# A pair-product batch norm: loads, shift, squares and root of its head rearranged

## The chip, the core and the metric

The kernel runs on one core of one Trainium2 chip. The metric is the device time of one execution in microseconds (us). The kernel before takes 1929.05 us, the median of three runs that lie between 1929.01 and 1929.15.

## The reference, cut to what matters

```python
# xi, xj: 1024 x 39 x 16; W: 1 x 16 x 16; 741 pairs (row > col)
cross = xj[:, rows, :, None] * xi[:, cols, None, :]          # 1024 x 741 x 16 x 16
mean = jnp.mean(cross, axis=(0, 2, 3), keepdims=True)        # one per pair
var = jnp.mean(jnp.square(cross - mean), axis=(0, 2, 3), keepdims=True)
normed = (cross - mean) * jax.lax.rsqrt(var + BN_EPS) * gamma + beta
out = normed * W
```

The output is 776.99 MB in float32, so that storing it takes nearly all the time. The statistics of a pair come from sums per field: both mean and variance follow from 39x39 matrices of products of sums of x and of x squared. To keep the variance exact, a shift per field is subtracted first.

## The kernel before

On each partition lie eight samples (t = 0 to 7). A head computes the statistics and at the same time prepares the first two output tiles as unscaled products. A long plateau then makes tile after tile: ScalarE and GpSimd multiply, VectorE adds and weighs with W, SP stores. The parts that the change and the argument touch:

```python
for t0 in range(0, NT, T):                                   # loads, two samples each
    nc.sync.dma_start(xj_sb[:, t0:t0+T], ...); nc.scalar.dma_start(xi_sb[:, t0:t0+T], ...)
nc.gpsimd.dma_start(w_sb[:, 0, :], ...)                      # W, on GpSimd's queue
# ... gamma on SP, beta on ScalarE's queue
sums(0)                                                      # VectorE: sums of samples 0, 1
emit(raw0, 8)                                                # ScalarE: eight products of tile 0
nc.scalar.copy(w_dve, w_sb)                                  # W to PSUM, for VectorE
# matmuls over the partitions -> shift (ScalarE)
for n in range(7): deviation(n)                              # GpSimd: x - shift
for n in range(8):
    square(n)                                                # ScalarE
    emit(raw0, 3)
    # ... VectorE: sums, moments(n), means(n); after two n: gram matmuls
emit(raw_products(1, nc.gpsimd, range(20, 32)), 12)
emit(raw1, 6)
# ... ScalarE: gram copies;  emit(raw1, 6);  VectorE: 15 steps on 39x39, reciprocal
nc.scalar.activation(rstd, inv, AF.Sqrt)                     # the root
emit(raw1, 8)
# ... VectorE: last steps; spread() by matmul to all partitions, then
#     st = ps * gamma ; st[1] = st[1] + beta    (the second: an addition with two SBUF inputs)
affine(0); weigh(0, FIRST_PIECES); scale_xi(2); spread(..); spread(..); affine(1); weigh(1, ..)
# ... three more spreads, then the loop over tiles: finish(2) is the first VectorE work of the plateau
```

`affine` alternates its 19 columns between ScalarE and GpSimd; `weigh` is VectorE's product with W, followed by a store of each piece.

## Time and profile before

| | kernel before |
|---|---|
| time | 1929.05 us |
| busy: VectorE, ScalarE, GpSimd | 90%, 86%, 79% of the span |
| DMA | busy without a break from 100 to 1650 us at 420 GB/s |
| first square on ScalarE | 15.59 us |
| gram copies | 37.84 us |
| affine operations, ScalarE | 45.88 us |
| third tile's finishing begins | 75.87 us |

Shares of busy time average over two stages with quite different limits, so they say little here. The DMA is the limit of the plateau. What a change of the head can win is how much earlier the plateau begins; this is the last line of the table. The prediction shows the lines.

### The profile page before, as it was taken

To read this page: it belongs to the slowest core of one execution; us is meant where nothing else is said; L and a number is where in the kernel's file an instruction comes from. 1 tells how busy PE (TensorE), PEld (TensorE's weight loads), DVE (VectorE), ACT (ScalarE), POOL (GpSimd) and SP (SyncE) were. 2 spreads that over 40 slices of the span, in tenths; PEclk is the share of its full clock that TensorE was granted. 3 is DMA by queue.
4 is the path that set the end of the run, shared out by engine and by line. 5 is a ranking of instruction groups with operands and counts; after the bars stand their busy time and mean duration, and the time that the engine had idled before them with its cause. 6 is when DMAs were issued, how large, how long until landed. Compare 5 with 4: busy or idle time off the path is not lost. (4 is left out here: it accounts for less than half of the span.)

```text
span 1927.5 us, 10086 instructions
## 1 busy us (share of the span) xinstructions
PE 25.5 (1%) x132; PEld 23.8 (1%) x132; DVE 1732.3 (90%) x2603; ACT 1663.4 (86%) x3690; POOL 1528.2 (79%) x1918
## 2 busy tenths in 40 slices
PE   2200000000000000000000000000000000000000
PEld 2200000000000000000000000000000000000000
DVE  5999999999989899999999999999999999888886
ACT  7999888888888988889888898888888888888752
POOL 6898888887878787979787878888888877777654
DMA  3799999999999999999999999999999999999998
GB/s 125 326 421 421 420 421 421 421 421 421 424 426 423 424 425 423 426 423 426 423 421 421 421 421 416 411 420 416 414 415 414 415 414 415 405 406 402 393 389 373
DMA packets 80174, 783.66 MB, mean 407 GB/s; under 512 B 4800, under 2 KB 5824, under 8 KB 14816
## 3 DMA queue, kind: packets, MB, share of 16 engines
q1 hardware_dynamic: 79328, 779.95, 96.8%
q10 hardware_dynamic: 720, 2.94, 0.4%
q14 instruction: 77, 0.63, 0.1%
q0 software_dynamic: 48, 0.13, 0.1%
q8 instruction: 1, 0.02, 0.0%
HBM read 6.00 MB, written 776.99 MB: 406 GB/s over the span
## 5 line engine op out<-in xcount | busy, mean ns | idle before, releaser
L222 DVE SCALAR_TENSOR_TENSOR y_sb<-y_sb,st_sb,w_dve 128x512 f32<-128x512 f32 x2542 | 1679.7, 742 | 158.5 <-issue 147.1
L130 ACT ACTIVATE y_sb<-xs,xj_sb 128x256 f32<-128x256 f32 (+33 forms) x3600 | 1613.4, 542 | 218.7 <-DMA out_dram<-y_sb 166.2
L132 POOL TENSOR_SCALAR y_sb<-xs,xj_sb 128x256 f32<-128x256 f32 (+33 forms) x1200 | 604.3, 527 | 198.5 <-DMA out_dram<-y_sb 131.3
L214 POOL TENSOR_TENSOR y_sb<-y_sb,w_sb 128x1024 f32<-128x1024 f32 (+4 forms) x138 | 441.8, 3202 | 11.5
L150 POOL TENSOR_TENSOR xs<-xi_sb,st_sb 128x576 f32<-128x576 f32 (+37 forms) x150 | 188.0, 1253 | 146.4 <-ACT y_sb L130 146.4
L210 POOL TENSOR_SCALAR y_sb<-y_sb,st_sb 128x512 f32<-128x512 f32 x384 | 259.6, 693 | 1.7 <-ACT y_sb L130 1.7
L130 ACT ACTIVATE y_sb<-xi_sb,xj_sb 128x304 f32<-128x304 f32 x52 | 23.9, 533 | 0.0
L191 DVE TENSOR_TENSOR y_sb<-y_sb,w_dve 128x5120 f32<-128x5120 f32 (+3 forms) x5 | 20.9, 4205 | 3.2 <-ACT y_sb L181 3.2
L183 POOL TENSOR_SCALAR y_sb<-y_sb,st_sb 128x512 f32<-128x512 f32 x18 | 13.5, 772 | 7.5 <-DVE st_sb L396 7.5
L383 PE MATMUL ps<-y_sb 39*128 39x38 f32 (+37 forms) x76 | 16.9, 398 | 20.1 <-DVE st_sb L390 13.9
L383 PEld LDWEIGHTS ps<-y_sb 39*128 39x128 f32 x76 | 16.4, 328 | 20.7 <-DVE st_sb L390 14.2
L281 DVE TENSOR_REDUCE y_sb<-y_sb 128x78 f32<-128x1248 f32 x8 | 11.6, 1448 | 3.8 <-ACT y_sb L275 3.6
L266 POOL TENSOR_TENSOR y_sb<-xj_sb,y_sb 128x1248 f32<-128x1248 f32 x4 | 9.3, 2321 | 6.3 <-ACT y_sb L319 6.3
L181 ACT ACTIVATE y_sb<-y_sb,st_sb 128x512 f32<-128x512 f32 x20 | 14.2, 798 | 0.0
L260 DVE TENSOR_REDUCE y_sb<-xj_sb 128x78 f32<-128x1248 f32 x4 | 5.8, 1449 | 8.5 <-DMA xj_sb<-in_r_xj_dram 8.5
L275 ACT ACTIVATE y_sb<-y_sb 128x1248 f32<-128x1248 f32 x8 | 9.8, 1228 | 2.2 <-POOL y_sb L266 2.2
L266 POOL TENSOR_TENSOR y_sb<-xi_sb,y_sb 128x1248 f32<-128x1248 f32 x4 | 9.3, 2318 | 0.0
L130 ACT ACT_TABLE_LOAD x1 | 1.3, 1283 | 7.8 <-DMA xi_sb<-in_r_xi_dram 7.8
L298 PE MATMUL ps_g<-y_sb 128*39 128x79 f32 x48 | 7.2, 339 | 18.6 <-DVE y_sb L286 18.6
L298 PEld LDWEIGHTS ps_g<-y_sb 128*39 128x39 f32 x48 | 6.1, 183 | 19.5 <-POOL y_sb L266 11.2
L132 POOL TENSOR_SCALAR y_sb<-xi_sb,xj_sb 128x304 f32<-128x304 f32 x12 | 5.9, 509 | 0.0
L260 DVE TENSOR_REDUCE y_sb<-xi_sb 128x78 f32<-128x1248 f32 x4 | 5.8, 1442 | 0.0
(42 smaller groups left out, 23.3 us busy)
## 6 DMA issues: line engine op xcount, KB each, us to landing
out_dram<-y_sb SPq DMA_DIRECT2D x56, 3072.0 KB, 11.7
out_dram<-y_sb SPq DMA_DIRECT2D x56, 2816.0 KB, 13.7
out_dram<-y_sb SPq DMA_DIRECT2D x52, 2560.0 KB, 14.2
out_dram<-y_sb SPq DMA_DIRECT2D x32, 3328.0 KB, 16.5
out_dram<-y_sb SPq DMA_DIRECT2D x16, 3584.0 KB, 17.8
out_dram<-y_sb SPq DMA_DIRECT2D x23, 2304.0 KB, 15.6
out_dram<-y_sb SPq DMA_DIRECT2D x20, 2048.0 KB, 22.4
out_dram<-y_sb SPq DMA_DIRECT2D x8, 1792.0 KB, 18.9
```

The lines of the kernel that those rows point to most:

```text
L130: nc.scalar.activation(y, src, AF.Copy, scale=scale)
L132: engine.tensor_scalar(y, src, scale, 1.0, ALU.mult, ALU.mult)
L150: nc.gpsimd.tensor_tensor(xs, xi_sb[:, t0 : t0 + T, 0:r, :], s_sb[:, :, n0 : n0 + r, :].to_broadcast([P, T, r, E]), ALU.mult,)
L181: nc.scalar.activation(y[:, :, c, :], y[:, :, c, :], AF.Identity, bias=t_c, scale=s_c)
L183: nc.gpsimd.tensor_scalar(y[:, :, c, :], y[:, :, c, :], s_c, t_c, ALU.mult, ALU.add)
L191: nc.vector.tensor_tensor(y[:, :, c0:c1, :], y[:, :, c0:c1, :], w_dve.unsqueeze(1).to_broadcast([P, T, c1 - c0, EE]), ALU.mult,)
L210: nc.gpsimd.tensor_scalar(y[:, :, c, :], y[:, :, c, :], t_sb[:, n0 + c : n0 + c + 1], 1.0, ALU.add, ALU.mult)
L214: nc.gpsimd.tensor_tensor(y[:, :, split:r, :], y[:, :, split:r, :], w_sb.unsqueeze(1).to_broadcast([P, T, r - split, EE]), ALU.mult,)
L222: stt(y[:, :, c, :], y[:, :, c, :], t_sb[:, n0 + c : n0 + c + 1], w_dve.to_broadcast([P, T, EE]), ALU.add, ALU.mult,)
L266: nc.gpsimd.tensor_tensor(devs[n % 7], sources[x][:, t0 : t0 + T], shift[:, x : x + 1, :].unsqueeze(3).to_broadcast([P, T, F, E]), ALU.sub ...
L298: nc.tensor.matmul(acc[0:F, 0 : 2 * F + 1], lhs, fb[:, t], start=t == 0, stop=t == NT - 1)
L383: nc.tensor.matmul(ps_v[:, :, first[r] - n0 : first[r] - n0 + r], pick[:, r, :], stq[:, :, 0:r], start=True, stop=True,)
```

## The change

The intent: let the statistics begin with the first sample alone (half-size first loads, shift from one sample), keep W's load from disturbing the loads of the fields, load only one activation table (an early dummy root brings in the table that also holds the copies and squares), and place products in ScalarE's gaps.

```diff
-FIRST_PIECES = (0, 3, 9, 19)
+FIRST_PIECES = (0, 2, 8, 19)
+LOADS = (0, 1, 2, 4, 6, 8)
...
-        for t0 in range(0, NT, T):
-            (loads of two samples)
-        nc.gpsimd.dma_start(w_sb[:, 0, :], ...)
+        for t0, t1 in zip(LOADS, LOADS[1:]):
+            (loads of t0 to t1)
+        nc.sync.dma_start(w_sb[:, 0, :], ...)
...
-        raw1 = raw_products(1, nc.scalar, range(20))
-        sums(0)
-        emit(raw0, 8)
-        nc.scalar.copy(w_dve, w_sb)
-        (shift from two samples)
+        raw1 = raw_products(1, nc.scalar, range(17))
+        nc.scalar.activation(shift_r, ones[0:F, 0:1], AF.Sqrt)
+        sums(0, 1)
+        (shift from one sample)
...
         for n in range(7):
             deviation(n)
+        emit(raw0, 4)
+        nc.scalar.copy(w_dve, w_sb)
         for n in range(2 * NT // T):
             square(n)
-            emit(raw0, 3)
+            emit(raw0, 4 if n < 4 else 3)
             (sums and means moved ahead)
-        emit(raw_products(1, nc.gpsimd, range(20, 32)), 12)
-        emit(raw1, 6)
+        emit(raw_products(1, nc.gpsimd, range(17, 32)), 15)
+        emit(raw1, 4)
         (gram copies)
-        emit(raw1, 6)
+        emit(raw1, 7)
         (39x39 steps, root)
-        emit(raw1, 8)
+        emit(raw1, 6)
```

More of the change, by code (lines that the diff above doesn't have):

```diff
@@ L232, in tile_pair_outer_batchnorm @@
     with tc.manual_schedule():
-        for t0 in range(0, NT, T):
-            nc.sync.dma_start(xj_sb[:, t0 : t0 + T], xj_v[:, t0 : t0 + T])
-            nc.scalar.dma_start(xi_sb[:, t0 : t0 + T], xi_v[:, t0 : t0 + T])
-        nc.gpsimd.dma_start(w_sb[:, 0, :], w.rearrange("o i j -> (o i j)").partition_broadcast(P))
+        for t0, t1 in zip(LOADS, LOADS[1:]):
+            nc.sync.dma_start(xj_sb[:, t0:t1], xj_v[:, t0:t1])
+            nc.scalar.dma_start(xi_sb[:, t0:t1], xi_v[:, t0:t1])
+        nc.sync.dma_start(w_sb[:, 0, :], w.rearrange("o i j -> (o i j)").partition_broadcast(P))
         nc.sync.dma_start(gb_all[:, 0], gamma.partition_broadcast(P))
@@ L246, in tile_pair_outer_batchnorm @@
         )
-        k_s = 1.0 / (T * P * E)
+        k_s = 1.0 / (P * E)
         batches = range(0, NT, T)
@@ L256, in part, with sums @@
             return slice(x * F, (x + 1) * F)
-        def sums(t0):
+        def sums(t0, t1):
             for x in range(2):
                 nc.vector.tensor_reduce(
-                    total[:, t0 : t0 + T, part(x)], sources[x][:, t0 : t0 + T], AX.X, ALU.add
+                    total[:, t0:t1, part(x)], sources[x][:, t0:t1], AX.X, ALU.add
                 )
@@ L302, in tile_pair_outer_batchnorm @@
         raw0 = raw_products(0, nc.scalar, range(32))
-        raw1 = raw_products(1, nc.scalar, range(20))
-        sums(0)
-        emit(raw0, 8)
-        nc.scalar.copy(w_dve, w_sb)
-        for t in range(T):
-            nc.tensor.matmul(
-                ps_s[:, 0 : 2 * F], ones, total[:, t], start=t == 0, stop=t == T - 1
-            )
-        for t in range(T):
-            nc.tensor.matmul(
-                ps_r[0:F, 0:1], total[:, t, 0:F], ones[:, 0:1], start=t == 0, stop=t == T - 1
-            )
+        raw1 = raw_products(1, nc.scalar, range(17))
+        nc.scalar.activation(shift_r, ones[0:F, 0:1], AF.Sqrt)
+        sums(0, 1)
+        nc.tensor.matmul(ps_s[:, 0 : 2 * F], ones, total[:, 0], start=True, stop=True)
+        nc.tensor.matmul(ps_r[0:F, 0:1], total[:, 0, 0:F], ones[:, 0:1], start=True, stop=True)
         nc.scalar.activation(
@@ L321, in tile_pair_outer_batchnorm @@
         nc.scalar.copy(ps_u, shift)
-        sums(2)
+        sums(1, 2)
+        means(0)
+        means(1)
         for n in range(7):
             deviation(n)
+        emit(raw0, 4)
+        nc.scalar.copy(w_dve, w_sb)
         for n in range(2 * NT // T):
             square(n)
-            emit(raw0, 3)
-            if n % 2 == 1 and n < 5:
-                sums(n + 3)
+            emit(raw0, 4 if n < 4 else 3)
+            if n % 2 == 0 and n < 6:
+                sums(n + 2, n + 4)
             moments(n)
@@ L332, in tile_pair_outer_batchnorm @@
                 deviation(7)
-            means(n)
+            if n % 2 == 0 and n < 6:
+                means(n + 2)
+                means(n + 3)
             if n % 2 == 1:
                 gram(n // 2 * T)
-        emit(raw_products(1, nc.gpsimd, range(20, 32)), 12)
-        emit(raw1, 6)
+        emit(raw_products(1, nc.gpsimd, range(17, 32)), 15)
+        emit(raw1, 4)
         for to, acc in zip((g1, g2, g3), ps_g):
```

## The prediction

> **What bounds the kernel now.** I first read the page's slices, then the table of engines and DMA by stretches of time. The core writes 776.99 MB, and between 100 and 1650 us the DMA engines are busy all the time at about 420 GB/s: that is the plateau. The time is therefore the length of the plateau and a tail, plus what comes before the stores flow without a gap. In the stretches, the columns after the engines are the clock, the share of DMA time and GB/s:
>
> ```profile
> 76.00:78.00 2.00, 0.00 (x0) 0.00 (x0) 2.00 (x4) 2.00 (x6) 2.00 (x5) 1.00 0.99 415
> 78.00:80.00 2.00, 0.00 (x0) 0.00 (x0) 2.00 (x4) 2.00 (x6) 2.00 (x3) 1.00 0.05 19
> 80.00:82.00 2.00, 0.00 (x0) 0.00 (x0) 2.00 (x4) 2.00 (x6) 1.92 (x3) 1.00 0.00 0
> 82.00:84.00 2.00, 0.00 (x0) 0.00 (x0) 2.00 (x4) 2.00 (x6) 2.00 (x3) 1.00 0.61 253
> ```
>
> See that the stores of the first two tiles run dry at 78 us, and nothing moves until the third tile's first piece is finished at about 82. So no earlier byte helps by itself: what counts is when VectorE begins the third tile's finishing operations (75.87 us in the timeline). From there it is 100% busy until 250 us. It makes 262 KB each 0.659 us (16 of them take 10.55 us between 75.87 and 86.4), 398 GB/s; GpSimd adds its 13% of the columns, so production barely exceeds the 421 GB/s that leave. **The end should move by as much as 75.87 moves.**
>
> Next, the timeline of the first 76 us, backwards from there. These lines carry it (start, length, engine, line, operation):
>
> ```profile
> 12.64 0.36 ACT L306 COPY w_dve<-w_sb 128x256 f32<-128x256 f32 x1
> 13.24 2.32 POOL L266 TENSOR_TENSOR y_sb<-xj_sb,y_sb 128x1248 f32<-128x1248 f32 x1 [6.25 <-ACT y_sb L319]
> 15.59 1.24 ACT L275 ACTIVATE y_sb<-y_sb 128x1248 f32<-128x1248 f32 x1 [2.17 <-POOL y_sb L266]
> ...
> 32.76 1.23 ACT L275 ACTIVATE y_sb<-y_sb 128x1248 f32<-128x1248 f32 x1
> ...
> 35.66 1.80 PE L298 MATMUL ps_g<-y_sb 128*39 128x79 f32 x12 [2.39 <-DVE y_sb L286]
> 37.84 0.45 ACT L344 ACTIVATE y_sb<-ps_g 39x79 f32<-39x79 f32 x3
> ...
> 40.94 1.28 ACT L368 ACT_TABLE_LOAD   x1
> 42.23 0.23 ACT L368 ACTIVATE y_sb<-y_sb 39x39 f32<-39x39 f32 x1
> ...
> 45.88 14.20 ACT L181 ACTIVATE y_sb<-y_sb,st_sb 128x512 f32<-128x512 f32 x20
> ...
> 53.13 5.49 DVE L191 TENSOR_TENSOR y_sb<-y_sb,w_dve 128x5120 f32<-128x5120 f32 x1 [0.17 <-ACT y_sb L181]
> ...
> 58.86 0.99 DVE L396 TENSOR_TENSOR st_sb<-st_sb,y_sb 128x66 f32<-128x66 f32 x1
> ```
>
> The reader is to see three stages. (1) Squares: GpSimd makes eight deviations (2.27 us apart), ScalarE squares each and puts three products behind it. The squares start every 2.455 us (15.59, 18.05, 20.50, ... 32.76), and ScalarE shows no wait after 15.59: ScalarE sets the pace, not GpSimd. (2) The small chain: gram products, the 39x39 steps, the root. (3) ScalarE's twenty affine operations start at 45.88 although their input was ready at 44.78: ScalarE was late with its products. From 53.13 VectorE has no wait of weight until 75, so 75.87 moves rigidly with it.
>
> **What the Trainium skill says.** "DMA: Bandwidth & Descriptors", section "Queues, rings and completion order": SP and ACT each own one ring on each of the same 16 DMA engines, and descriptors are consumed in ring order. The trace agrees: gamma was issued behind the fields at 7.28 us and took 11.9 us, to 19.2, whereas DMA work had ended at about 18.4; so a small load waits for all before it, and a landing shows 0.8 us after the last byte. "ScalarE: Activation LUTs", section "What ACT_TABLE_LOAD costs": about 1283 ns for the load, plus a drain of about 1380 ns. The trace shows 1.28 us, and the next operation 1.29 us after the load's start (40.94 to 42.23): no further drain is visible here, so I use 1.29. "SBUF — State Buffer", section "Who interferes with whom": a VectorE operation with two SBUF inputs is blocked by a GpSimd operation that reads SBUF. The 0.99 us at 58.86 agrees: a like addition on 110 elements, more than its 66, took 0.28 us at 60.17; GpSimd was in its affine operations until 59.66.
>
> **The change, part by part.**
>
> *Loads.* The first loads are halves (0.32 MB each). In the trace 0.205 MB have moved by 3.0 us, and the rate is then some 415 GB/s, so the first pair (0.64 MB) is through at about 4.1 and lands at 4.9 instead of 7.3. Sums over one sample are half as long (0.72 for 1.44 us), shift's matmuls halve, and GpSimd could start its deviations at about 8.7 rather than 13.24. I take 8.7 because beta's issue on ScalarE waits for the second xi load (1.28 MB through at 5.6, landing 6.45), and then come the table load (1.28) and a small root. This gain of 4.5 us is real on GpSimd, but GpSimd is not what paces.
>
> *W behind the fields.* In the new order of ScalarE the copy of W into PSUM stands **before the first square**. W is now on SP's ring behind all of xj, and its issue also waits for the second xj load. The fields are 8 x 0.639 = 5.11 MB: 3.0 + (5.11 - 0.205)/0.415 = 14.8 us. W (0.13 MB) comes then, interleaved with beta (0.38 MB): 0.3 to 1.2 us, plus 0.8 for landing: 15.9 to 16.8, I choose 16.4. In the kernel before, W went by GpSimd's queue and was there at 9.2 (1.3 + 7.9), so its copy at 12.64 waited for nothing. So ScalarE should stand still from about 10.8 to 16.45, and the first square should start 0.30 us later (12.64 to 12.94 before): 16.75, against 15.59. **+1.16.** The early start of everything in front of it is lost in that wait.
>
> *Products moved.* Eight products stood before the shift; now four stand before the copy, and the first four squares have four products behind them, not three: 4 x 0.44 us (eight took 3.53) = **+1.75** in the paced stage. The last square starts at 32.76 + 2.91 = 35.67 and ends at 36.9.
>
> *Behind the last square.* Before, ScalarE had nine products left there (4.04 us) and reached the gram copies at 37.84, just after the gram products (35.66 + 1.80). Now seven are left and the wait is for data: 36.9 + 0.02 + 1.45 (last reduction) + 0.1 + 1.80 + 0.1 = 40.37. The means between reductions and matmuls are gone from there (0.2 us, already left out). Gram copies: 40.37 against 37.84.
>
> *Small chain.* From gram copies to the affine operations it was 45.88 - 37.84 = 8.04 us. Now: copies 0.35, seven products 3.20 (six took 2.74), root 0.14 (VectorE's side is ready after 3.07), six products 2.63, in all 6.32; the input is ready at 3.55 + 2.55 + 0.18 = 6.28. So 6.35: **-1.7** from the table load removed (1.29) and ScalarE's later group cut by two products (0.88), less one product more before the root. Affine operations at 46.72, **+0.85**.
>
> *First pieces.* 2, 6 and 11 columns for 3, 6 and 10. The first store leaves about a microsecond earlier relative to the affine start, which the dry spell at 78 us swallows. The last piece is 5632 elements instead of 5120 and stands on the path: by the slope between 1536 (1.75 us) and 5120 (5.49), 6.02 us: **+0.53**.
>
> *Port.* GpSimd's affine chain before led ScalarE's by 0.92 us; now both start together, so GpSimd ends at about 61.3 (46.6 + 14.7) and the addition that ended at 59.85 is blocked until about then: at most 0.3 more; I take **+0.1**.
>
> Sum: +0.85 + 0.53 + 0.1 = +1.5 us; 1929.05 + 1.5 = 1930.5.
>
> **The rivals.** (a) *W is there in time* (its ring is served sooner than I think, or its packets overtake). Then the first square comes right behind the first deviation, 11.1; the last starts at 11.1 + 4 x 2.90 + 3 x 2.455 = 30.1, gram copies at 34.8, affine at 41.1; -4.8 + 0.6 = -4.2: 1924.9. The change's intent speaks for it; gamma's landing after the fields speaks against it. (b) *The loads are no faster.* In the kernel before, the rate fell to 75 GB/s between 6 and 7 us and 197 between 7 and 8; I put this down to W's own 48 packets on GpSimd's queue, so that it goes. If it stays, W lands 1.5 us later: 1932.0. (c) *The head is hidden* by the plateau: 1929.05. The dry spell at 78 to 82 us speaks against it: no store is then in stock.
>
> **Range and chances.** The fields' 5.11 MB can't land much before 15.5 us, which puts the low end at about -0.4 us; (b) and a later W give the high end. I choose 1928.6 to 1932.2. 2% is 39 us, more than ten times all of this: same 0.985, faster 0.005, slower 0.01.
>
> **What would show it.** In the new timeline: ScalarE's copy of W at about 16.4 us, released by a DMA, with ScalarE idle some 5.5 us before it; the first square at 16.7 and the fifth at 28.4 (2.9 us apart), the last at 35.7; gram copies at 40.4 behind PE; no second table load; affine at 46.7; the third tile's finishing at 77.4. It is wrong if the copy runs at 11 us (then look for the gain in full at 75.87), or if 75.87 moves and the end doesn't.

## The result, and the profile after

The changed kernel takes 1931.45 us (median of six runs, 1931.31 to 1932.05), the kernel before in the same rounds 1929.10. The ratio is 1.0013, with a 95% interval of 1.0 to 1.0026. A ratio here is the mean time of one kernel's fast runs over that of the other's of the same rounds, so not quite the ratio of the medians. By the 2% rule this is "same"; by its own spread it is about 2.3 us slower: the six times of each kernel lie within 0.75 us and do not overlap. The prediction was 1930.5 in a range of 1928.6 to 1932.2.

The timeline of the changed kernel, the lines that answer to those of the prediction (start, length, engine, line, operation, and in brackets the idle time before it and what ended that):

```profile
9.01 2.32 POOL L268 TENSOR_TENSOR y_sb<-xj_sb,y_sb 128x1248 f32<-128x1248 f32 x1 [3.31 <-ACT y_sb L315]
...
17.23 0.38 ACT L324 COPY w_dve<-w_sb 128x256 f32<-128x256 f32 x1 [6.24 <-DMA w_sb<-in_L_rec_W_dram]
17.54 1.24 ACT L277 ACTIVATE y_sb<-y_sb 128x1248 f32<-128x1248 f32 x1
...
36.46 1.23 ACT L277 ACTIVATE y_sb<-y_sb 128x1248 f32<-128x1248 f32 x1
...
39.23 1.80 PE L300 MATMUL ps_g<-y_sb 128*39 128x79 f32 x12 [2.71 <-DVE y_sb L283]
40.66 0.63 ACT L346 ACTIVATE y_sb<-ps_g 39x79 f32<-39x79 f32 x3
...
44.27 0.22 ACT L370 ACTIVATE y_sb<-y_sb 39x39 f32<-39x39 f32 x1
...
46.99 3.76 POOL L185 TENSOR_SCALAR y_sb<-y_sb,st_sb 128x512 f32<-128x512 f32 x5 [12.33 <-DVE st_sb L398]
47.03 3.62 ACT L183 ACTIVATE y_sb<-y_sb,st_sb 128x512 f32<-128x512 f32 x5
...
60.53 1.33 DVE L398 TENSOR_TENSOR st_sb<-st_sb,y_sb 128x66 f32<-128x66 f32 x1
...
77.61 23.12 DVE L224 SCALAR_TENSOR_TENSOR y_sb<-y_sb,st_sb,w_dve 128x512 f32<-128x512 f32 x35
```

GpSimd begins its deviations 4.2 us earlier than before (9.01 for 13.24). ScalarE, which must square them, stands for 6.24 us before the copy of W, and the bracket names W's load as what it waited for. The first square comes at 17.54, two microseconds later than before. There is one table load less, and the root follows the gram copies by 3.61 us instead of 4.39. The third tile's finishing starts at 77.61, 1.74 us later than before.

The dry spell of the stores has moved with it (stretches; the last two columns are the DMA share and GB/s):

```profile
80.00:82.00 2.00, 0.00 (x0) 0.00 (x0) 2.00 (x4) 2.00 (x6) 2.00 (x4) 1.00 0.05 21
82.00:84.00 2.00, 0.00 (x0) 0.00 (x0) 2.00 (x4) 2.00 (x6) 1.92 (x2) 1.00 0.00 0
84.00:86.00 2.00, 0.00 (x0) 0.00 (x0) 2.00 (x4) 2.00 (x6) 2.00 (x3) 1.00 0.71 295
```

The plateau has the same rates in both (421 GB/s from 100 to 250 us, 420 from 250 to 1650). A VectorE group that began at 1615.93 now begins at 1617.65, still 1.72 us later. The rest of the 2.35 us arises after that, in the tail.

### The profile page after: what moved, and what is told of

Its sections match the earlier page's. It is cut to its first block, busy times and chain, and to the rows that moved or that the text cites. A ratio compares the mean times of both kernels' runs of the same rounds, so it can differ in the third digit from the quotient of the medians.

```text
span 1929.6 us, 10085 instructions
## 1 busy us (share of the span) xinstructions
PE 25.0 (1%) x128; PEld 23.2 (1%) x128; DVE 1732.6 (90%) x2605; ACT 1661.0 (86%) x3687; POOL 1528.7 (79%) x1920
## 5 line engine op out<-in xcount | busy, mean ns | idle before, releaser
L193 DVE TENSOR_TENSOR y_sb<-y_sb,w_dve 128x1024 f32<-128x1024 f32 (+4 forms) x5 | 20.9, 4204 | 2.9 <-ACT y_sb L183 2.0
L385 PEld LDWEIGHTS ps<-y_sb 39*128 39x128 f32 x76 | 16.4, 328 | 19.1 <-DVE st_sb L392 14.2
L262 DVE TENSOR_REDUCE y_sb<-xj_sb 128x78 f32<-128x1248 f32 (+1 forms) x5 | 5.9, 1187 | 5.0 <-DMA xj_sb<-in_r_xj_dram 5.0
L307 ACT ACT_TABLE_LOAD x1 | 1.3, 1283 | 7.3 <-DMA xi_sb<-in_r_xi_dram 7.3
L262 DVE TENSOR_REDUCE y_sb<-xi_sb 128x78 f32<-128x1248 f32 (+1 forms) x5 | 5.9, 1182 | 0.0
## 6 DMA issues: line engine op xcount, KB each, us to landing
out_dram<-y_sb SPq DMA_DIRECT2D x23, 2304.0 KB, 15.6
```

The lines of the kernel that those rows point to most:

```text
L193: nc.vector.tensor_tensor(y[:, :, c0:c1, :], y[:, :, c0:c1, :], w_dve.unsqueeze(1).to_broadcast([P, T, c1 - c0, EE]), ALU.mult,)
L385: nc.tensor.matmul(ps_v[:, :, first[r] - n0 : first[r] - n0 + r], pick[:, r, :], stq[:, :, 0:r], start=True, stop=True,)
```

## The experiments

Each kernel was timed in five rounds beside the kernel before on the same chip; all gave correct results. The summary first (profiled run: times of the events in us; the last column is the span less the finishing's start):

| run | copy of W | first square | gram copies | affine, ScalarE | finishing | time, median | ratio | span less finishing |
|---|---|---|---|---|---|---|---|---|
| before | 12.64 | 15.59 | 37.84 | 45.88 | 75.87 | 1929.05 | | 1851.6 |
| changed | 17.23 | 17.54 | 40.66 | 47.03 | 77.61 | 1931.45 | 1.0013 | 1852.0 |
| e1 copy late | 32.78 | 11.40 | 34.84 | 41.01 | 71.60 | 1925.39 | 0.9981 | 1852.1 |
| e2 W on GpSimd's queue | 12.93 | 13.40 | 36.53 | 42.89 | 73.47 | 1927.15 | 0.9990 | 1852.0 |
| e3 before, W behind | 16.77 | 19.74 | 41.99 | 50.04 | 79.74 | 1932.57 | 1.0018 | 1851.3 |
| e4 products early | 17.14 | 17.46 | 38.82 | 45.19 | 75.77 | 1929.66 | 1.0003 | 1852.1 |
| e5 old pieces | 17.67 | 17.98 | 41.11 | 47.47 | 78.04 | 1931.53 | 1.0011 | 1852.0 |
| e6 two tables | 16.75 | 17.07 | 40.19 | 47.98 | 78.56 | 1932.29 | 1.0015 | 1851.9 |
| e8 before, new pieces | 12.82 | 15.77 | 38.02 | 46.07 | 76.06 | 1929.31 | 0.9999 | 1851.5 |
| e9 affine split | 17.29 | 17.60 | 40.72 | 47.09 | 76.95 | 1930.80 | 1.0007 | 1852.1 |
| e7 balanced | 39.94 | 11.38 | 32.33 | 42.45 | 73.23 | 1927.04 | 0.9989 | 1852.2 |
| e10 balanced, split | 39.85 | 11.45 | 32.39 | 42.37 | 71.61 | 1925.43 | 0.9980 | 1852.1 |
| e11 before, split loads | 13.94 | 16.89 | 39.15 | 47.19 | 77.20 | 1931.09 | 1.0009 | 1852.3 |
| e12 small steps in PSUM | 36.92 | 11.17 | 32.11 | 39.42 | 68.72 | 1922.56 | 0.9964 | 1852.0 |

The last column is what the prediction's main step claims: between finishing starts that lie 11 us apart it varies by 1 us. To within that, the span moves with that start, one for one. Where W is loaded behind the fields, the copy's time varies by 0.9 us from run to run (16.75 to 17.67), so effects below a microsecond are read from the timeline, relative to it. The runs are of four jobs, in which the kernel before had medians of 1929.06 (e1 to e4), 1929.40 (e5, e6, e8, e9), 1929.21 (e7, e10, e11) and 1929.59 us (e12); medians of different jobs compare to a few tenths only.

### e1: the copy of W behind the last square

```diff
         emit(raw0, 4)
-        nc.scalar.copy(w_dve, w_sb)
         for n in range(2 * NT // T):
...
         emit(raw_products(1, nc.gpsimd, range(17, 32)), 15)
+        nc.scalar.copy(w_dve, w_sb)
```

> The changed kernel with one line moved: ScalarE's copy of W into PSUM stands behind the last square instead of before the first. My theory (ScalarE's wait of 6.24 us for W sets the squares back): the first square starts right behind the first deviation, at about 11.4 us (17.54 in the changed kernel); the gram copies then start at 34.5 (40.66), the affine operations at 40.9 (47.03), the third tile's finishing at 71.5 (77.61), and the time falls by the same 6.1 us, to about 1925.3. Rival 1 (GpSimd or the loads pace the squares anyway): the first square still starts after 15 us and the time stays at 1931.4. Rival 2 (the plateau of stores hides the head): the timeline moves, the time stays at 1931.4.

Measured: 1925.39 us (1925.15 to 1925.47), ratio 0.9981 with an interval of 0.9968 to 0.9993. One line moved is worth 6.1 us. The timeline of this run:

```profile
11.40 1.24 ACT L277 ACTIVATE y_sb<-y_sb 128x1248 f32<-128x1248 f32 x1 [0.38 <-POOL y_sb L268]
...
34.84 0.45 ACT L346 ACTIVATE y_sb<-ps_g 39x79 f32<-39x79 f32 x3
```

The first square now waits 0.38 us for GpSimd's deviation and not for W. Everything behind it is 6 us earlier, to the end. Both rivals fall: neither GpSimd nor the loads set the pace, and the plateau does not hide the head.

### e2: W on GpSimd's queue, as before

```diff
-        nc.sync.dma_start(w_sb[:, 0, :], ...)
+        nc.gpsimd.dma_start(w_sb[:, 0, :], ...)
```

> The changed kernel with W loaded from GpSimd's queue as in the kernel before, all else as changed. My theory: W lands at about 9.2 us and ScalarE's copy, at about 11, waits for nothing; the first square starts at 11.4 to 12.6, depending on whether W's packets bring back the dip in the load rate between 6 and 8 us (if so the second xi load lands some 1.5 us later, and with it the table load, the shift and the deviations). Time 1925.3 to 1926.6. Rival (moving W away from GpSimd's queue is what pays): no better than 1931.4, as the loads get slower by as much as the copy gets earlier.

Measured: 1927.15 us (1926.71 to 1927.45), half a microsecond above the range expected. The copy waits for nothing, but the change's motive for moving W is real as well. The load rates by the microsecond, of the kernel before, of e2 and of the changed kernel:

```profile
6.00:7.00 1.00, 0.00 (x0) 0.00 (x0) 0.00 (x0) 0.00 (x0) 0.98 (x1) 1.00 0.81 75
```

```profile
6.00:7.00 1.00, 0.29 (x2) 0.32 (x2) 0.56 (x1) 0.00 (x0) 0.98 (x1) 1.00 1.05 101
```

```profile
6.00:7.00 1.00, 0.38 (x2) 0.41 (x2) 1.00 (x2) 0.00 (x0) 0.00 (x0) 1.00 1.02 419
...
15.00:16.00 1.00, 0.00 (x0) 0.00 (x0) 0.00 (x0) 0.00 (x0) 1.00 (x2) 1.00 0.92 258
16.00:17.00 1.00, 0.00 (x0) 0.00 (x0) 0.00 (x0) 0.00 (x0) 1.00 (x1) 1.00 0.97 340
```

With W on GpSimd's queue the rate falls to 75 and 101 GB/s, though the DMA engines are busy; without it, 419. The second sample of xj is summed from 8.37 us in e2 and from 6.39 in the changed kernel. So W's small load on GpSimd's queue costs some 2 us of the fields' time. The packets in the kept traces fit this: W's 32 packets of 4 KB there took a median of 0.86 us each in e2, its 128 packets of 1 KB on SP's queue 0.05 us each in the changed kernel. No run loads W early on another queue, so whether the queue or the early place counts is not shown. Behind the fields, on SP's queue, the changed kernel has a second dip (258 and 340 GB/s). It does not come with W's load as such: with the same loads of W, beta and gamma, e3 moves 409 and 372 GB/s in these two microseconds and e6 406 and 399. What makes this dip is open. Against e1, which has W behind the fields and the copy late, e2 is 1.8 us slower. W behind the fields was right; its copy in front of the squares was not.

### e3: the kernel before, with W behind the fields and nothing else

```diff
-        nc.gpsimd.dma_start(w_sb[:, 0, :], ...)
+        nc.sync.dma_start(w_sb[:, 0, :], ...)
```

> The kernel before with W's load alone moved to SP's queue behind the fields. There the copy of W stands before the shift, so that all of it waits. My theory: W lands at about 17.0 us, the copy starts there (12.64 before), the shift follows, GpSimd's first deviation starts at 17.7 (13.24) and the first square at 20.1 (15.59); time 1929.1 + 4.5 = 1933.6. Rival (W behind the fields speeds the fields up and costs nothing): 1929.1 or less.

Measured: 1932.57 us (1932.36 to 1932.92), 3.5 us slower. The direction is as expected, the size is a microsecond less: W was there at 16.77 and not 17.0, and the first square 4.15 us later instead of 4.5. Finishing starts 3.87 us later. The rest of the difference lies in the tail (last column of the table) and is not explained.

### e4: four more products in the wait, four fewer in the squares

```diff
-        emit(raw0, 4)
+        emit(raw0, 8)
...
-            emit(raw0, 4 if n < 4 else 3)
+            emit(raw0, 3)
```

> The changed kernel with eight products instead of four before the copy of W, in the time in which ScalarE waits for W anyway, and three instead of four behind each of the first four squares. My theory (ScalarE paces the squares): the squares come every 2.455 us throughout, the last starts 1.75 us earlier, 34.7 (36.46), and the time falls by 1.7 us to about 1929.7. Rival (GpSimd's deviations pace the squares): the last square stays at 36.5 and the time at 1931.4.

Measured: 1929.66 us (1929.37 to 1930.02). The last square starts at 34.62 (36.46) and the time falls by 1.8 us. ScalarE paces the squares. The four moved products cost 1.75 us in one place and nothing in the other, where ScalarE waits anyway.

### e5 and e8: the first pieces

e5 is the changed kernel with `FIRST_PIECES = (0, 3, 9, 19)`, e8 the kernel before with `(0, 2, 8, 19)`.

> The changed kernel with the first pieces back at 3, 6 and 10 columns. My prediction's sum put +0.53 us on the path for the longer last piece: then the third tile's finishing starts at 77.1 (77.61) and the time is 1930.9. Rival, from the traces of both kernels (the addition behind that piece is held until GpSimd's affine run ends, 61.66 us, however early VectorE gets there): it still ends at about 61.9, finishing starts at 77.6 and the time stays at 1931.4. Third possibility: the 0.65 us by which the changed kernel and its kin end later after that start than the kernel before (start to end 1853.8 against 1853.2 or less) come from the pieces; then the start stays at 77.6 but the time is 1930.8.

> The kernel before with the first pieces of the change alone, 2, 6 and 11 columns. By my prediction's sum: finishing starts 0.53 us later, 76.4 (75.87), time 1929.6. By the theory of the held addition: VectorE gets to it at 59.4 instead of 58.86, it still ends when GpSimd's run ends, 59.85, finishing stays at 75.9 and the time at 1929.1. If the pieces cause the 0.65 us after that start: finishing 75.9, time 1929.7.

Measured: e5 1931.53 us (1931.52 to 1931.68), e8 1929.31 (1929.12 to 1929.34; the kernel before beside it had 1929.40). The pieces make no difference either way, and my +0.53 us is wrong. In e5, VectorE's addition after the last piece and GpSimd's row around it:

```profile
55.36 6.76 POOL L185 TENSOR_SCALAR y_sb<-y_sb,st_sb 128x512 f32<-128x512 f32 x9
60.45 1.86 DVE L398 TENSOR_TENSOR st_sb<-st_sb,y_sb 128x66 f32<-128x66 f32 x1
```

The addition of 66 elements lasts from 60.45 to 62.31. GpSimd's nine affine operations end at 62.12. In the changed kernel it began later relative to them, lasted 1.33 us and ended as much after their end; in the kernel before it lasted 0.99, in e8 0.46. In all fourteen kernels it ended 0.2 us after GpSimd's row ended, whenever it had begun. VectorE's shorter last piece only buys a longer hold.

### e9: GpSimd's row shortened by one operation

```diff
-            if c % 2 == 0:
+            if c % 2 == 0 or c >= keep:
...
-        affine(1)
+        affine(1, 17)
```

> The changed kernel with one of GpSimd's nine affine columns of the second tile given to ScalarE, so that GpSimd's unbroken run ends 0.75 us earlier, at 60.9. Theory of the held addition: the addition that VectorE reaches at 60.53 ends at 61.1 (61.86), finishing starts at 76.9 (77.61), time 1930.7. Rival (something else makes that addition slow): it ends at 61.9 and the time stays at 1931.4, or grows by up to 0.7 as ScalarE's affine run gets longer.

Measured: 1930.80 us (1930.70 to 1931.06).

```profile
54.98 6.01 POOL L185 TENSOR_SCALAR y_sb<-y_sb,st_sb 128x512 f32<-128x512 f32 x8
60.59 0.62 DVE L398 TENSOR_TENSOR st_sb<-st_sb,y_sb 128x66 f32<-128x66 f32 x1
```

GpSimd's row ends at 60.99 and the addition at 61.21. Finishing starts at 76.95, 0.66 us earlier, and the time is 0.65 lower. So it is GpSimd's row that holds the addition, and that row is on the path.

### e6: two table loads

```diff
-        nc.scalar.activation(shift_r, ones[0:F, 0:1], AF.Sqrt)
```

> The changed kernel without the early root, so that the table for the root is loaded just before the late root again. My theory: the load (1.28 us) stands on the path there; the root starts at 45.5 (44.27), the affine operations at 48.3 (47.03), time 1931.45 + 1.3 = 1932.7. With a further drain of about 1.4 us, as the Trainium skill has it, 1934.1. Rival (the load is hidden while ScalarE waits for the reciprocal, which ends at 43.9): 1931.4 to 1931.9.

Measured: 1932.29 us (1932.06 to 1932.39). In this profiled run W's copy came 0.48 us sooner than in the changed kernel's; counted from it, the affine operations start 1.43 us later (31.23 for 29.80) and so does the finishing.

```profile
43.91 1.28 ACT L369 ACT_TABLE_LOAD   x1
45.20 0.23 ACT L369 ACTIVATE y_sb<-y_sb 39x39 f32<-39x39 f32 x1
```

The load stands fully on the path: the root follows its start by 1.29 us, with no further drain. The medians differ by only 0.84 us, less than the 1.3 that I expected; they are of two jobs (the kernel before had 0.3 us more in this one, which leaves some 0.5), and W's landing varies by as much.

### e7 and e10: ScalarE's work spread anew

Both have the copy of W later still than e1, behind the root, and the old pieces, 21 raw products on GpSimd instead of 15, and 43 on ScalarE instead of 49. e10 gives two of GpSimd's affine columns to ScalarE as well. The core of the edit:

```diff
-        raw1 = raw_products(1, nc.scalar, range(17))
+        raw1 = raw_products(1, nc.scalar, range(11))
...
-        emit(raw0, 4)
-        nc.scalar.copy(w_dve, w_sb)
+        emit(raw0, 5)
...
-            emit(raw0, 4 if n < 4 else 3)
+            emit(raw0, 3 if n < 6 else 2)
...
-        emit(raw_products(1, nc.gpsimd, range(17, 32)), 15)
+        emit(raw_products(1, nc.gpsimd, range(11, 32)), 21)
...                                     # e10 also: affine(1, 15), with e9's edit
         nc.scalar.activation(rstd, inv, AF.Sqrt)
+        nc.scalar.copy(w_dve, w_sb)
```

> A version that should beat both: the changed kernel with the copy of W behind the root, where ScalarE waits for the affine input; ScalarE's raw products cut from 49 to 43, with 21 instead of 15 on GpSimd, and placed 5 before the squares, 3 behind each of the first six squares, 2 behind the last two, 5 + 6 + 5 in the later waits; first pieces 3, 6, 10. By my theory: squares start at 11.4, the last at 28.1, gram copies at 32.3, affine operations at 38.7; VectorE's held addition ends with GpSimd's affine run, at about 53.5; third tile's finishing 69.3 (77.61), time 1923.1. Rival (GpSimd's longer row of products, to 37.6 us by the theory, delays its affine start): finishing later by as much as GpSimd is late, and the time 1924 to 1925.

> As e7, and two of GpSimd's nine affine columns of the second tile go to ScalarE, so that GpSimd's run ends 1.5 us earlier. Theory of the held addition: it is no longer held for long, finishing starts 1.4 us earlier than in e7, 67.9, and the time is 1921.7. Rival (nothing held by then): the same as e7, or later by up to 1.4 us for ScalarE's longer run.

Measured: e7 1927.04 us (1927.00 to 1927.16), e10 1925.43 (1925.21 to 1925.77). The step from one to the other is 1.6 us, as the held addition demands. But both are some 4 us slower than expected. Up to the gram copies all was as planned (32.33 us). The loss lies in the 39x39 steps. e10:

```profile
27.33 10.48 POOL L134 TENSOR_SCALAR y_sb<-xi_sb,xj_sb 128x304 f32<-128x304 f32 x21
...
32.79 3.19 DVE L352 SCALAR_TENSOR_TENSOR y_sb<-y_sb 39x39 f32<-39x39 f32 x1 [1.89 <-ACT y_sb L345]
...
35.91 0.58 DVE L353 SCALAR_TENSOR_TENSOR y_sb<-y_sb 39x39 f32<-39x39 f32 x1
36.41 0.51 DVE L354 TENSOR_SCALAR y_sb<-y_sb 39x39 f32<-39x39 f32 x1
```

A step that lasts 0.25 us in the kernel before took 3.19 us. The four behind it took half a microsecond each, one GpSimd product apiece, until GpSimd's 21 products ended at 37.8. One of these four, at 36.41, has a single tensor as input (a product with the constant 2, from SBUF to SBUF); it takes 0.17 us in the kernel before. In the changed kernel the 15 products were over (34.65 us) before the steps began (41.06), so that this didn't show. I had not thought of it when I gave GpSimd more.

### e12: the same, with the small steps between SBUF and PSUM

```diff
-    g1, g2, g3 = (scratch("rest", F, 2 * F + 1) for _ in range(3))
-    k, mean, q1, q2, var, rstd, inv = (scratch("rest", F, F) for _ in range(7))
+    g2, g3 = (scratch("rest", F, 2 * F + 1) for _ in range(2))          # SBUF
+    q1, kk, ks, rstd = (scratch("rest", F, F) for _ in range(4))        # SBUF
+    g1 = ps_r[0:F, 2 : 2 * F + 3]                                       # PSUM
+    k, mean, q2, var, inv, qp = (ps_r[0:F, ...] for x in range(6))      # PSUM
...
+        stt(ks, v, e_a, k, ALU.mult, ALU.add)                           # k once more, to SBUF
         stt(k, v, e_a, k, ALU.mult, ALU.add)
...     # each step reads one tensor from SBUF and the other from PSUM
```

> As e10, and the small 39x39 steps are arranged so that each reads at most one tensor from SBUF and the other from PSUM (one step more). Why: in e7 and e10 the first of these steps took 3.19 us and the next four 0.5 us each, until GpSimd's 21 products ended at 37.8 us; the reciprocal ended at 39.7 instead of 35.1. Theory of the held operation with two SBUF inputs: the first step takes 0.25 us though GpSimd is in its products, the reciprocal ends at about 36.1, the affine operations start at 39.0 (42.37), the third tile's finishing at 68.3 (71.61), time 1922.1. Rival (VectorE is slowed by GpSimd's products in another way, or PSUM operands make the steps slow): finishing stays at 71 to 72 and the time at 1925.

Measured: 1922.56 us (1922.47 to 1922.80), ratio 0.9964 with an interval of 0.995 to 0.9977, against 1929.59 for the kernel before in the same rounds.

```profile
27.05 10.38 POOL L139 TENSOR_SCALAR y_sb<-xi_sb,xj_sb 128x304 f32<-128x304 f32 x21
...
32.51 0.26 DVE L358 SCALAR_TENSOR_TENSOR ps_r<-ps_r,y_sb 39x39 f32<-39x39 f32 x1 [1.89 <-ACT y_sb L350]
...
33.47 0.25 DVE L361 SCALAR_TENSOR_TENSOR y_sb<-y_sb,ps_r 39x39 f32<-39x39 f32 x1
...
36.32 0.41 DVE L375 RECIPROCAL ps_r<-ps_r 39x39 f32<-39x39 f32 x1
```

The same first step beside the same GpSimd products takes 0.26 us. So a step with two SBUF inputs is held, and with one of them in PSUM it is not. The result's place does not matter here: the step at 33.47 writes to SBUF and takes 0.25. Two SBUF inputs are not the only case, though. The product with the constant, which was held in e10 with one SBUF input, has both sides in PSUM in e12 (0.20 us at 33.17), so that the gain is that of both moves together. Affine operations start at 39.42 (39.0 expected) and finishing at 68.72 (68.3). This version is 7.0 us faster than the kernel before by the medians of its rounds, the fastest.

### e11: the kernel before with split loads

```diff
-        for t0 in range(0, NT, T):
+        for t0, t1 in zip(LOADS, LOADS[1:]):      # LOADS = (0, 1, 2, 4, 6, 8)
```

> The kernel before with its first loads split into one sample each, nothing else. All kernels of the changed kind end 0.55 us later after the start of the third tile's finishing than those of the kind before (1852.0 against 1851.5 us in the profiled runs), and the difference arises after 1616 us. If the two further loads cause it (another place in the round of load and store semaphores): start unchanged at 75.9 to 76.1, from there to the end 1852.0, time 1929.7. If not: 1851.5 and 1929.1 to 1929.3.

Measured: 1931.09 us (1930.65 to 1931.21), 1.9 us slower than the kernel before. The start of the finishing I got wrong: it is 1.33 us later (77.20). W is still on GpSimd's queue, and the second half of the first samples now comes behind its packets: the first sums start at 8.38 us instead of 7.28. From there to the end it takes 1852.3 us, like the changed kernels and unlike those without split loads. So the slower tail comes with the split loads alone. By which mechanism stays open; a kernel with as many loads but another order would be needed to tell.

## Why the prediction was right, and where its terms were off

**The cause** was right. "W behind the fields" put the wait where the prediction put it: ScalarE stood for 6.24 us (about 5.5 predicted) before the copy, and e1 shows that taking away the wait is worth the whole 6.1 us. The early start of GpSimd was lost in it, as said. Rival (a), W in time, is what e1 makes true: the first square at 11.40 (11.1 predicted) and 1925.39 us (1924.9 predicted). Rival (b), loads no faster, falls by the 419 GB/s between 6 and 7 us, and rival (c), the plateau hides the head, by all runs.

**W's landing** was sized at 16.4 us and measured at 17.2. The fields came as computed. In the two microseconds behind them the rate was 258 and 340 GB/s where I had assumed 415 (why is open, see e2). W's last packet ended at 16.77, where my sum had 15.6 and 0.8 for the landing; the copy started 0.46 us behind it. The 0.8 us was read too long: gamma's last packet in the kernel before ended at 18.72, 0.5 us ahead of its landing at 19.2. The first square is +1.95 us against the +1.16 predicted.

**Products moved**: +1.75 predicted; the last square went from +1.95 to +3.70, so 1.75, and e4 gave 1.8 back.

**Gram copies**: 40.37 predicted, 40.66 measured, although the last square was 0.8 us late. I had counted all twelve gram matmuls before the first copy, as a wait for data. That wait did not come: ScalarE shows none from 30 to 46 us. It came to the copies straight from its seven products (37.59 to 40.75), and they begin at 40.66 while the matmuls run to 41.03. So ScalarE set the pace here as well.

**Table load**: my sum took 1.29 us away for it, and e6 shows that it does stand on the path. But from the gram copies to the root only 0.78 us were won (3.61 for 4.39). With one product more in front of it, ScalarE came to the root at 44.27, while the reciprocal had ended at 43.87. The prediction's 3.55 for this stretch held.

**The small chain, the pieces and the port** added up right, but for wrong reasons. I followed ScalarE's affine start (+0.85 predicted, +1.15 measured) and added the longer last piece (+0.53) and a little for the port (+0.1). The path does not go there. It goes from the affine input, which GpSimd takes up at once, through GpSimd's row, to the addition that is held until that row ends. GpSimd's start went from 44.96 to 46.99, +2.03, and the end of the held addition from 59.85 to 61.86, +2.01. So ScalarE's two products fewer behind the root (0.88 us in my sum) win nothing, and the pieces cost nothing (e5, e8). That the sum still came near is luck. The prediction had seen the hold, and its own figure for the end of GpSimd's row, 61.3 us for 59.66, gives +1.6 by this path; but it allowed 0.3 and took 0.1. Its comparison, the addition at 60.17 (0.28 us), also ran beside GpSimd, whose products had begun at 59.64; it began 0.05 us before the end of one. What counts in that stretch is the gain up to the root, 0.78 us (3.61 for 4.39 after the gram copies). GpSimd's two rows in the kernel before and the second in the changed kernel:

```profile
44.96 6.76 POOL L183 TENSOR_SCALAR y_sb<-y_sb,st_sb 128x512 f32<-128x512 f32 x9 [7.55 <-DVE st_sb L396]
...
52.89 6.77 POOL L183 TENSOR_SCALAR y_sb<-y_sb,st_sb 128x512 f32<-128x512 f32 x9
```

```profile
54.92 6.76 POOL L185 TENSOR_SCALAR y_sb<-y_sb,st_sb 128x512 f32<-128x512 f32 x9
```

The sum as measured: +1.95 (W), +1.75 (products), -0.88 (fewer products in front of the gram copies: 4.20 us from last square to copies, 5.08 before), -0.78 (table), -0.03, and -0.27 (a later addition of 245 elements took 0.41 us for 0.70). That makes +1.74 us, the shift of the finishing, against +1.5 predicted. The last term, in the kernel before and in the changed one:

```profile
75.25 0.70 DVE L396 TENSOR_TENSOR st_sb<-st_sb,y_sb 128x245 f32<-128x245 f32 x1
```

```profile
77.27 0.41 DVE L398 TENSOR_TENSOR st_sb<-st_sb,y_sb 128x245 f32<-128x245 f32 x1
```

This addition, too, runs beside GpSimd's products. In both kernels it ends 0.3 us after the end of the product under way, at 75.69 and 77.35, and it happened to begin 0.4 and 0.1 us before that end. No run changes this alone, but the code is not the reason: e3, of the kind before, has 0.41 as well.

**After that start** I expected no difference. The medians differ by 2.35, which leaves 0.6 us in the tail; it comes with the split loads (e11) and its mechanism is open. So "the end should move by as much as 75.87 moves" is true to about half a microsecond, no better.

## What to carry to other kernels

A load that is moved to the back of a queue takes with it whatever waits for it in an in-order engine: move the consumer too, to the last place where it is still early enough. One operation with two SBUF inputs on VectorE (in e10 also one with a single SBUF input) can make the length of a GpSimd row part of the critical path; look for VectorE operations that last several times as long as their like, and see whether they end together with a GpSimd row. Then give one operand a place in PSUM, or shorten the row, before trimming anything else on VectorE.

## What the Trainium skill lacked or had wrong

- "SBUF — State Buffer", section "Who interferes with whom": the rule that a VectorE operation with two SBUF inputs is blocked by a GpSimd operation that reads SBUF holds here. It lacks that the hold can outlast one GpSimd operation. The first small step in e10 took 3.19 us beside products of 0.5 us each, and the addition in e5 1.86 us beside operations of 0.75. In all fourteen kernels, the addition ended 0.2 us after the end of GpSimd's whole row. The addition of 245 elements waited for one product only; what decides between the two is open.
- "ScalarE: Activation LUTs", section "What ACT_TABLE_LOAD costs": the 1283 ns agree (1.28 us). The further drain of about 1380 ns shows nowhere here: the next operation starts 1.29 us after the load in the kernel before and in e6, and e6's affine operations come 1.43 us later, not 2.66.
- "DMA: Bandwidth & Descriptors": no section says what a small load on GpSimd's queue costs the loads beside it. W's 0.13 MB there brought the rate from some 415 GB/s down to 75 (kernel before) and 101 (e2) for a microsecond, with packets of a median of 0.78 and 0.86 us. On SP's queue its packets of a quarter of that size took 0.05 us, and the rate was 406 and 399 GB/s in e6, but 258 and 340 in the changed kernel.
